# A 65-column first transform, a rearranged loading tail and filter checks moved into the mixers, in an attention and convolution network on one core

## The chip, the core and the metric

The kernel runs on one core of a Trainium2 chip. Five engines with queues of their own work side by side: PE (TensorE, matrix products), DVE (VectorE), ACT (ScalarE), POOL (GpSimd) and SP (SyncE, which here issues DMAs). An engine takes up its own instructions in order; semaphores tie the engines together. The metric is the device time of one execution in microseconds. Every operand is fp32, and each fp32 product shows in the trace as two PE records, each with a weight load before it.

## The reference, cut to what matters

The input x has 4 batches of 32 images of 128 x 128. Two layers follow each other, and each adds to x first a mixing over the image and then a recurrent network over the rows. Layer 0's mixing is an attention whose maps are spectral convolutions; layer 1's is a filtered leaky ReLU.

```python
# layer 0
x = x + conv0(ln_c(x), ...)              # the attention below
t = to_tokens(x); t = t + ffn0(ln_t(t))  # scan of yt = sigmoid(wx_t + yt @ V.T)
# layer 1
x = x + conv1(ln_c(x), bias, up, dn)     # up-filter, leaky ReLU, down-filter
t = to_tokens(x); t = t + ffn1(ln_t(t))

def codano_forward(x, ...):
    tokens = x.reshape(b * t, 1, H, W)
    tokens_norm = instance_norm(tokens, norm1_g, norm1_b)
    k = fno_layer(tokens_norm, key_w, ..., (H // 2, W // 2))
    q = fno_layer(tokens_norm, query_w, ..., (H // 2, W // 2))
    v = fno_layer(tokens_norm, value_w, ..., (H, W))
    dprod = softmax(einsum('bhtd,bhsd->bhts', qf, kf) / scale)
    attn = einsum('bhts,bhsd->bhtd', dprod, vf)
    attn = instance_norm(fno_layer(attn, proj_w, ...) + tokens, ...)
    m = fno_layer(instance_norm(attn, ...), mixer_w1, ..., norm=..., act=gelu)
    m = fno_layer(m, mixer_w2, ..., norm=...)
    return instance_norm(m, ...) + attn
```

An `fno_layer` is a 1x1 convolution, resampled to the output's shape, plus a product with weights on a few low frequencies between two Fourier transforms. Only 32 by 17 frequencies are ever used, so the transforms are products with small tables.

## The kernel before

All 128 images lie in SBUF as `XA` (partition: image row). The stages follow each other: loading and first transform with the attention scores (to about 137 us), attention applied (`mix`, `SUMS`, `NORMS`), the two mixers (`MIXERS`, an order written out by hand, run for eight chunks of four tokens), the first scan, the convolutions of layer 1 with their features, and the second scan.

**Loading.** Image loads go out on SP in pieces of eight images (512 KB, `load`). For each half batch k (16 images, eight in all) `stats(k, n)` takes row statistics on DVE (L823) and turns them into factors `r` and `nmr` (L385 to L390, L375 to L380, with one square root on ACT, L376). `transform(k)` normalises the images in place, ACT or DVE by the image's number (`normalise`, L845 and L847), multiplies each by a table of 130 columns in `cst` (L862), copies three images' results at a time from PSUM to `A1` (L863), multiplies `A1` by further tables into `pfs`, the low frequencies (L870), and into `ps_pr`, a half-size image in a rotated basis (L874, L876), which ACT copies to `Rn` (L879), and sends the normalised images to the DRAM tensor `normed` (L881).

**Scores.** `scores(b)` copies `pfs` to `FF` (L888), turns it on DVE (L889), replicates it through PE (L895, L896), multiplies it with the weights on DVE (L902 to L924), transposes on PE (L931, L932) and forms the scores `psc` (L936). `gram(b)` forms the products of `Rn` (L947, L952). `scales` prepares factors (L962 to L988), and `attend(b)` is the softmax (L1001 to L1020), which ends with one block of `CTbd`. `weights` prepares the weights (L621 to L736). Each is a generator; the loops over k step them between pieces of `transform`.

**Order.** In a `with in_order()` block every instruction of PE, DVE, ACT and POOL is tied to the one traced before it on its engine. Outside such blocks a scheduler places the instructions by a cost model, so one traced late can land early in a queue if its inputs seem to be there; `ndcm` (L717), which needs only the constants, is one. Transforms 0 and 1 and the tail are in order; transforms 2 to 7 are not. After transform 7 SP issues eight loads that bring `normed` back into `XA`, now with rows on another axis (L1071), and then runs this order:

```python
with in_order():
    for work in (scoring, extra, extra, extra, scoring, scoring, scoring, products, products, scoring, scoring,
                 scoring, scoring, scoring, extra, extra, scoring):
        step(work)
    through(scoring, extra, attend(NB - 1))
```

`extra` is `filters()`: for both of layer 1's filters it checks that the two-dimensional filter is an outer product (L759 to L785, counts in `ok`) and lays out its taps (L789 to L805). The taps go to a DRAM tensor `hankel` (L807), cleared before (L748); both are read only in layer 1. The first `mix` product (L1092) needs all of `CTbd` and the first reloaded rows.

**Mixers.** Each piece of `MIXERS` is a function with a chunk's number. M4c ends a chunk's weights on DVE (L1565, L1566), FHG transforms them back on PE (L491), Z forms the next images on DVE (L1418), g is a GELU on ACT (L1423), R adds up the result on DVE (L1586, L1587), and FS and BN take statistics (L1597, L459). The PSUM tile with the tag "t" in the pool `psf` has one buffer.

Of the kernel before, what the change touches and what calls it, by code (L numbers as in the profile page):

```python
# [26 lines left out]
F32 = mybir.dt.float32  # L27
AF = mybir.ActivationFunctionType
ALU = mybir.AluOpType
# [125 lines left out]
    IRI0.2 M4b.1 de.1 M4c.1 FHG.1 gBc.1 g3.2 Z0.2 FS2.0 Z1.2 g2.2 QG0.1 FS1.0 FS0.0 g1.2 g0.2 ST2.2 A2.2 sq2.2 FS3.0  # L155
    IRS0.1 TA1.1 ZS2.2 AF.0 sq3.2 ST0.2 QG1.1 PW.0 ZS3.2 ZD.2 A0.2 TA0.1 PF.2 sq0.2 R1a.1 sq1.2 LD2.1 FZ.2 SQ.2
    R0b.1 R0a.1 FHIa.3 R1b.1 AO.0 IRS2.1 M1.2 TA2.1 LD0.2 FHIb.3 R2b.1 XN1a.0 XN0b.0 PS.2 M2.2 TA3.1 QI0.3 XN0a.0
    PG1.2 XN1b.0 QI1.3 R2a.1 PG2.2 XT0.0 M2b.2 IRI2.3 R3a.1 R3b.1 XC0.0 XT1.0 P2.2 IRI0.3 Z2.3 M3.2 Z3.3 WX0.0 XC1.0
    P3.2 XN2a.0 al.2 Z0.3 M4a.2 g2.3 M4b.2 g3.3 Z1.3 g0.3 de.2 GB.2 M4c.2 BN0.0 g1.3 FS2.1 FS1.1 ZS2.3 ST2.3 sq1.3
    sq2.3 FHG.2 ST0.3 QG0.2 XN3b.0 IRS0.2 A2.3 A0.3 TA1.2 gBc.2 TA0.2 XN2b.0 FS3.1 PF.3 sq0.3 FS0.1 WC0.0 XT2.0  # L160
    ZS3.3 QG1.2 sq3.3 WX1.0 FZ.3 ZD.3 R1b.2 AF.1 R0b.2 IRS2.2 SQ.3 TA3.2 XC2.0 PW.1 R0a.2 PG1.3 R1a.2 M1.3 BN1.0
    LD2.2 PS.3 TA2.2 R3a.2 XN3a.0 WC1.0 M2.3 AO.1 WX2.0 R2a.2 FHIa.4 BN2.0 R3b.2 PG2.3 XN0b.1 FHIb.4 M2b.3 XT3.0
    P2.3 XN0a.1 M3.3 WC2.0 al.3 QI0.4 R2b.2 QI1.4 P3.3 XC3.0 IRI0.4 XN1a.1 XT0.1 Z1.4 M4a.3 IRI2.4 WX3.0 XN1b.1 Z0.4
    XC0.1 g1.4 M4b.3 de.3 g0.4 M4c.3 Z3.4 Z2.4 GB.3 FHG.3 BN3.0 FS3.2 g3.4 FS1.2 FS2.2 LD0.3 QG0.3 ST0.4 g2.4 FS0.2
    gBc.3 A0.4 QG1.3 ZS3.4 ZS2.4 IRS0.3 sq1.4 TA1.3 sq2.4 ST2.4 LD2.3 R1a.3 TA0.3 A2.4 WC3.0 PF.4 R1b.3 XN2b.1 FZ.4
    AF.2 ZD.4 XT1.1 sq3.4 R0b.3 WX0.1 IRS2.3 PW.2 R0a.3 SQ.4 sq0.4 PG1.4 TA2.3 XC1.1 M1.4 PS.4 BN0.1 TA3.3 AO.2 M2.4
    M2b.4 R2b.3 XN3a.1 XN2a.1 WC0.1 XT2.1 FHIa.5 R3b.3 LD0.4 R3a.3 XC2.1 P2.4 XN3b.1 XN0b.2 M3.4 PG2.4 XN0a.2 P3.4
    FHIb.5 QI0.5 QI1.5 XT3.1 WX1.1 IRI0.5 al.4 R2a.3 XN1a.2 XC3.1 BN1.1 M4a.4 Z1.5 IRI2.5 de.4 WC1.1 M4b.4 M4c.4
    XN1b.2 FS0.3 GB.4 gBc.4 WX2.1 XT0.2 BN2.1 g1.5 XN2b.2 Z3.5 WC2.1 FHG.4 FS3.3 XC0.2 QG0.4 WX3.1 FS1.3 FS2.3 QG1.4
    LD2.4 XT1.2 XN2a.2 XN3a.2 IRS0.4 XC1.2 TA1.4 BN3.1 Z2.5 TA0.4 AF.3 g2.5 Z0.5 R1b.4 XT2.2 IRS2.4 g0.5 WC3.1  # L170
    FHIa.6 sq0.5 R1a.4 R0a.4 R0b.4 WX0.2 ZS2.5 PW.3 g3.5 ZS3.5 BN0.2 TA2.4 AO.3 FHIb.6 ZD.5 ST2.5 sq2.5 FS0.4 R2b.4
    XN3b.2 ST0.5 XC2.2 sq1.5 R2a.4 sq3.5 WC0.2 A0.5 TA3.4 WX1.2 R3b.4 BN1.2 A2.5 PF.5 QI0.6 IRI0.6 XN0a.3 R3a.4
    XN0b.3 XT3.2 Z0.6 WC1.2 FZ.5 SQ.5 M1.5 QI1.6 PG1.5 XC3.2 g0.6 Z1.6 IRI2.6 PS.5 Z2.6 M2.5 g1.6 WX2.2 Z3.6 g2.6
    g3.6 P2.5 BN2.2 M2b.5 M3.5 XN1a.3 XT0.3 FS2.4 PG2.5 P3.5 FS3.4 XC0.3 ST0.6 al.5 M4a.5 WC2.2 A0.6 ST2.6 de.5
    M4b.5 M4c.5 WX0.3 A2.6 BN0.3 XN1b.3 PF.6 ZS2.6 sq0.6 ZS3.6 sq3.6 FS1.4 GB.5 FZ.6 FHG.5 WC0.3 SQ.6 QG0.5 WX3.2
    sq2.6 AF.4 IRS0.5 TA0.5 PW.4 PG1.6 sq1.6 gBc.5 XT1.3 QG1.5 M1.6 XC1.3 LD0.5 ZD.6 BN3.2 TA1.5 R0a.5 XN2a.3 R0b.5
    PS.6 LD2.5 AO.4 IRS2.5 M2.6 XN3b.3 XN2b.3 TA3.5 WC3.2 XT2.3 P2.6 M2b.6 XN3a.3 WX1.3 XC2.3 R1a.5 PG2.6 XT3.3
    TA2.5 R1b.5 FHIa.7 FHIb.7 XN0a.4 R3a.5 BN1.3 M3.6 R2a.5 XN0b.4 XC3.3 WC1.3 WX2.3 XN1b.4 QI0.7 R2b.5 XT0.4 P3.6
    QI1.7 R3b.5 al.6 BN2.3 M4a.6 de.6 XN1a.4 IRI0.7 IRI2.7 XN2b.4 XC0.4 WC2.3 Z1.7 LD0.6 M4b.6 WX3.3 g1.7 XT1.4
    M4c.6 BN3.3 FHG.6 XC1.4 WC3.3 WX0.4 Z0.7 Z2.7 FS2.5 g0.7 FS0.5 g2.7 GB.6 Z3.7 FS1.5 QG0.6 ST0.7 g3.7 BN0.4  # L180
    IRS0.6 FS3.5 A0.7 sq0.7 ZS2.7 TA1.6 ST2.7 gBc.6 ZS3.7 XN2a.4 ZD.7 WC0.4 QG1.6 A2.7 TA0.6 XT2.4 PF.7 R1b.6 sq1.7
    R1a.6 sq3.7 LD2.6 WX1.4 AF.5 FZ.7 R0a.6 SQ.7 XN3b.4 IRS2.6 PW.5 R0b.6 PG1.7 sq2.7 TA2.6 M1.7 LD0.7 XC2.4 PS.7
    AO.5 XN0a.5 XN3a.4 BN1.4 WC1.4 XN0b.5 R2a.6 M2.7 R2b.6 TA3.6 XT3.4 XN1a.5 XC3.4 WX2.4 R3b.6 M2b.7 P2.7 PG2.7
    XN1b.5 BN2.4 WC2.4 XT0.5 M3.7 WX3.4 R3a.6 al.7 P3.7 BN3.4 M4a.7 de.7 XC0.5 LD2.7 FS2.6 M4b.7 XT1.5 XN2b.5 XC1.5
    GB.7 WC3.4 M4c.7 FS3.6 XN2a.5 gBc.7 WX1.5 BN1.5 WC1.5 FS0.6 XT2.5 FHG.7 WX0.5 QG0.7 FS1.6 XN3b.5 AF.6 BN0.5
    IRS0.7 WC0.5 TA0.7 R0a.7 QG1.7 XC2.5 TA1.7 PW.6 XN3a.5 TBL.7 WX2.5 XT3.5 IRS2.7 R1a.7 AO.6 BN2.5 XN0b.6 TA2.7
    XC3.5 XN0a.6 R0b.7 WC2.5 R1b.7 XN1b.6 XT0.6 XN1a.6 XC0.6 FS1.7 FS0.7 WX3.5 AF0.7 XT1.6 BN3.5 TA3.7 XN2b.6 R2a.7
    R2b.7 XN3b.6 WC3.5 WX0.6 XN2a.6 XC1.6 XN3a.6 XT2.6 WX1.6 XC2.6 BN0.6 PW0.7 XT3.6 FS2.7 AO0.7 WC0.6 R3b.7 R3a.7
    WX2.6 BN1.6 XN02a.7 XN00a.7 FS3.7 XN00b.7 XC3.6 XN02b.7 WC1.6 WX3.6 XT02.7 XT00.7 XC02.7 XC00.7 AF2.7 WX02.7
    BN2.6 BN3.6 WC2.6 WC3.6 PW2.7 AO2.7 XN20b.7 WX00.7 XN22b.7 XN20a.7 XN22a.7 XT20.7 BN02.7 BN00.7 XC20.7 XT22.7  # L190
    XC22.7 WX20.7 BN20.7 WC00.7 WC02.7 WX22.7 BN22.7 WC20.7 WC22.7
# [15 lines left out]
C_E = 0  # L207

C_DW = C_E + 130
C_CR = C_DW + 96  # L210
C_SW = C_CR + 128
C_EH2 = C_SW + 256
# [19 lines left out]
def _constants():  # L232
    c = np.zeros((P, C_N), np.float64)
# [14 lines left out]
    basis = np.concatenate([(h2[:, None] % 2 == np.arange(2)) / np.sqrt(32), np.cos(turn) / np.sqrt(32),  # L248
                            np.sin(turn) / np.sqrt(32)], 1)
    c[:, C_E + 64 : C_E + 128] = rows.real.T @ basis  # L250
    c[:, C_E + 128 : C_E + 130] = (rows.imag.T @ basis)[:, :2]
# [3 lines left out]
    c[:, C_CR : C_CR + 64] = cols.real  # L255
    c[:, C_CR + 64 : C_CR + 128] = -cols.imag
# [30 lines left out]
def _network(  # L287
# [94 lines left out]
    def row_stats(st, n, mean, var):  # L382

        d = sm([P, NG], "rw_d")[:, :n]
        tt(mean, st[:, :, 1], st[:, :, 4], ALU.add)  # L385
        ts(mean, mean, 0.5, None, ALU.mult)
        tt(d, st[:, :, 1], st[:, :, 4], ALU.subtract)
        stt(d, d, 0.25, d, ALU.mult, ALU.mult)
        tt(var, st[:, :, 2], st[:, :, 5], ALU.add)
        stt(var, var, 1.0 / P, d, ALU.mult, ALU.add)  # L390
# [169 lines left out]
    s4 = aw.tile([P, NB], F32, name="s4")  # L560
    ndcm = aw.tile([P, 1], F32, name="ndcm")
# [28 lines left out]
    nc.sync.dma_start(cst[:, :C_SW], consts[:, :C_SW])  # L590
# [6 lines left out]
    if redo is not None:  # L597
        for k in range(2):
            F = wp.tile([2 * PAD + 1, 2, 12], F32, name=f"F{k}")
            taps_in.append(F)  # L600
            for j in range(2):
                f = up[j, 0] if k == 0 else dn[j]
                nc.gpsimd.dma_start(F[:, j, :], f[P // 2 - PAD : P // 2 + PAD + 1, :, P // 2])
    nc.sync.dma_start(cst[:, C_SW:], consts[:, C_SW:])
# [10 lines left out]
    def weights():  # L615
# [101 lines left out]
        ts(ndcm, dcm, -1.0, 1.0, ALU.mult, ALU.add)  # L717
# [21 lines left out]
    def filters():  # L739

        n = 2 * PAD + 1
# [4 lines left out]
        taps = wp.tile([1, 8, n], F32, name="taps")  # L750
        for k in range(2):
            F = taps_in[k]

            def small_(shape, name):
                return wp.tile(shape, F32, tag=name, name=name)


            fsq = small_([n, 3, 12], "fsq")
            tt(fsq[:, 0, :], F[:, 0, :], F[:, 1, :], ALU.add)  # L759
            tt(fsq[:, 1:3, :], F, F, ALU.mult)  # L760
            tt(fsq[:, 1, :], fsq[:, 1, :], fsq[:, 2, :], ALU.add)
            rsum = small_([n, 2], "rsum")
            nc.vector.tensor_reduce(rsum, F, AX.X, ALU.add)
            rows = small_([n, n, 2], "frows")
            tt(rows, ident[0:n, 0:n].unsqueeze(2).broadcast_to([n, n, 2]),
               rsum.unsqueeze(1).broadcast_to([n, n, 2]), ALU.mult)
            yield True
            p = big("ps_f")
            mm(p[:n, 0:24], ones_sq[0:n, 0:n], fsq[:, 0:2, :].rearrange("p a b -> p (a b)"), start=True, stop=True)
            mm(p[:n, 24 : 24 + 2 * n], ones_sq[0:n, 0:n], rows.rearrange("p a b -> p (a b)"), start=True, stop=True)  # L770
            sums = small_([n, 24 + 2 * n], "sums")
            nc.vector.tensor_copy(sums, p[:n, : 24 + 2 * n])
            yield True
            total = small_([n, 2], "total")
            nc.vector.tensor_reduce(total, sums[:, :24].rearrange("p (a b) -> p a b", a=2), AX.X, ALU.add)
# [1641 lines left out]
```

## Time and profile before

| what | us |
|---|---|
| three runs, median (lowest to highest) | 870.35 (870.03 to 872.82) |
| the profiled execution, its own time | 870.38 |
| its span, first to last instruction | 868.6 |
| PE, DVE, ACT, POOL busy | 750.8, 710.9, 649.4, 361.2 |
| PE's first product of transform 0 | 18.22 |
| first product of transform 1, 2 | 35.37, 47.91 |
| image reload issued, first `mix` product | 111.64, 136.83 |

PE's share of busy time is 86%, DVE's 82%, ACT's 75%: no engine alone sets the end, so gains have to be looked for in the stretches where a chain of single steps or one engine does. Matmuls are pipelined and a record of one contains its latency, so PE's real occupancy is read from runs of equal products (the length of a run of 16 against a run of 2), not from the mean duration. The page's slices of the span show PE, DVE and ACT near nine tenths in most of loading and the mixers. The time of a DMA issue and that of its landing are different records; a wait for several semaphores is put down to the one that came last.

### The profile page before, as it was taken

The page shows a single profiled execution, that of the slowest core. Times are in us where ns is not written, and L with a number is a line of the kernel's source. Part 1 is how long each engine was busy: PE and PEld are TensorE (multiplying, and loading weights), DVE is VectorE, ACT ScalarE, POOL GpSimd, SP SyncE. Part 2 cuts the span into 40 slices and gives each one's busy share as a digit, 9 for nine tenths or more (in the row PEclk, how much of TensorE's full clock was granted, in tenths as well). Part 3 has the DMA queues.
Part 4 walks back from the last instruction along what each step waited for, and adds up shares of the span by engine and source line. Part 5 has one row for each costly group of instructions (what it writes and reads, how often), then busy time and mean ns, then how long its engine had stood idle before and what let it go on. Part 6 is the DMA issues. An engine that isn't in the chain of part 4 may idle for free.

```text
span 868.6 us, 31057 instructions
## 1 busy us (share of the span) xinstructions
PE 750.8 (86%) x12550; PEld 560.5 (65%) x12550; DVE 710.9 (82%) x2330; ACT 649.4 (75%) x1669; POOL 361.2 (42%) x604
## 2 busy tenths in 40 slices
PE   1799967977878999899779979999999999998994
PEld 1566633336645555645349968888788877875994
DVE  3789668976598899899889978977878877677996
ACT  2588934585738689989779977887777887776994
POOL 2000000011435444365310016788788786961263
PEclk9799967996789899999999969999999999999998
DMA  9954992349611011120000000111111111118454
GB/s 224 260 153 94 250 366 103 137 204 276 162 51 49 26 49 35 42 73 25 25 1 1 1 3 17 40 41 40 28 41 28 41 28 40 40 40 291 172 186 148
DMA packets 105130, 83.22 MB, mean 96 GB/s; under 512 B 5457, under 2 KB 98129, under 8 KB 102865
## 3 DMA queue, kind: packets, MB, share of 16 engines
q1 hardware_dynamic: 104641, 80.86, 31.2%
q8 instruction: 101, 1.65, 0.8%
q0 software_dynamic: 288, 0.01, 0.2%
q14 instruction: 52, 0.43, 0.2%
q10 hardware_dynamic: 48, 0.26, 0.1%
HBM read 47.46 MB, written 33.66 MB: 93 GB/s over the span
## 4 chain that ended last, share of the span: by engine, by line
PE 44%; DVE 25%; ACT 14%; POOL 9%; issue 5%; DMA 1%; SPq 1%; DVEq 0%; ACTq 0%; POOLq 0%
PE ps_k L2068 5%; PE ps_scan L1915 4%; DVE XA L1587 4%; PE ps_d L2198 4%; ACT WXY L1917 4%; DVE XA L1586 4%; PE ps_st L862 3%; ACT yw L1917 3%; POOL XN L2047 3%; PE pm L1092 3%; PE ps_st L1429 3%; PE ps_r L2068 2%; PE ps_e L2205 2%; PE ps_y L1299 2%; POOL xn L2047 2%
## 5 line engine op out<-in xcount | busy, mean ns | idle before, releaser
L2188 DVE SCALAR_TENSOR_TENSOR U<-raw 128x512 f32<-128x512 f32 x128 | 89.8, 731 | 27.8 <-ACT raw L2180 27.6
L1916 DVE SCALAR_TENSOR_TENSOR ps_scan<-WXY,bs,ps_scan 128x128 f32<-128x128 f32 x376 | 105.5, 352 | 1.8 <-PE ps_scan L1915 0.8
L2068 PE MATMUL ps_k<-WXY,q 64*64 64x134 f32 x2048 | 86.0, 282 | 0.9 <-ACT WXY L2152 0.3
L2180 ACT COPY raw<-ps_k 128x512 f32<-128x512 f32 x128 | 71.0, 597 | 17.0 <-PE ps_k L2068 14.6
L2198 PEld LDWEIGHTS ps_d<-WXY,U 128*64 128x64 f32 x2048 | 66.7, 137 | 19.5 <-issue 12.1
L2047 POOL TENSOR_SCALAR XN<-XA,c_r,c_o 128x128 f32<-128x128 f32 x120 | 74.7, 631 | 5.0 <-issue 2.2
L2047 POOL TENSOR_SCALAR xn<-XA,f_r,f_o 128x128 f32<-128x128 f32 x120 | 67.2, 569 | 18.1 <-PE ps_x L2068 12.1
L2198 PE MATMUL ps_d<-WXY,U 128*64 128x67 f32 x2048 | 73.4, 224 | 1.2 <-ACT q L2211 0.9
L2068 PEld LDWEIGHTS ps_k<-WXY,q 64*64 64x64 f32 x2048 | 60.7, 135 | 6.4 <-DVE U L2188 0.8
L862 PE MATMUL ps_st<-cst,XA 128*128 128x130 f32 x256 | 42.8, 313 | 24.9 <-ACT XA L845 22.1
L2068 PE MATMUL ps_r<-WXY,XN 64*64 64x134 f32 x1024 | 59.0, 290 | 2.8 <-DVE XN L2047 1.3
L862 PEld LDWEIGHTS ps_st<-cst,XA 128*128 128x128 f32 x256 | 35.9, 212 | 29.1 <-ACT XA L845 23.1
L1644 ACT ACTIVATE xn<-XA,f_o,f_r 128x128 f32<-128x128 f32 x120 | 51.0, 489 | 4.6 <-DVE f_o L1626 3.4
L1423 ACT ACTIVATE Z<-Z,k,aB 128x128 f32<-128x128 f32 x128 | 51.0, 480 | 4.2 <-DVE Z L1418 4.0
L1586 DVE SCALAR_TENSOR_TENSOR XA<-ps_inv,r1B,xin 128x128 f32<-128x128 f32 x128 | 44.1, 345 | 8.1 <-PE ps_inv L1579 8.1
L1587 DVE SCALAR_TENSOR_TENSOR XA<-Z,gB,XA 128x128 f32<-128x128 f32 x128 | 46.3, 362 | 5.0
L2166 ACT COPY q<-ps_r 128x512 f32<-128x512 f32 x64 | 38.2, 597 | 13.2 <-PE ps_r L2068 12.8
L2027 POOL TENSOR_TENSOR c_r<-c_e,neg_half 128x16 f32<-128x16 f32 (+2 forms) x10 | 25.6, 2563 | 53.3 <-DVE c_e L2020 53.1
L506 PE MATMUL ps_inv<-invq,cst 64*128 64x512 f32 x128 | 41.4, 674 | 3.9 <-ACT invq L497 3.2
L456 PE MATMUL ps_wx<-xt,wvt 128*128 128x512 f32 x64 | 35.9, 643 | 6.7 <-ACT WXY L463 5.5
L845 ACT ACTIVATE XA<-XA,p_n,p_r 128x128 f32<-128x128 f32 x80 | 35.4, 491 | 7.6 <-DVE p_n L829 7.6
L2205 PE MATMUL ps_e<-WXY,q 128*64 128x67 f32 x1024 | 40.8, 222 | 0.0
(441 smaller groups left out, 2100.8 us busy)
## 6 DMA issues: line engine op xcount, KB each, us to landing
XA<-in_x_dram SPq DMA_DIRECT2D x16, 512.0 KB, 7.2
normed<-XA SPq DMA_DIRECT2D x8, 1024.0 KB, 6.1
XA<-normed SPq DMA_DIRECT2D x8, 1024.0 KB, 10.4
mixed<-XA SPq DMA_DIRECT2D x8, 1024.0 KB, 3.8
XA<-mixed SPq DMA_DIRECT2D x32, 256.0 KB, 5.3
xin<-in_x_dram SPq DMA_DIRECT2D x32, 256.0 KB, 3.3
turned<-XA SPq DMA_DIRECT2D x32, 256.0 KB, 2.5
out_dram<-res SPq DMA_DIRECT2D x52, 128.0 KB, 2.1
```

Source lines behind the costliest of these rows:

```text
L862: mm(p[:, i, :], XA[:, b, t0 + j + i, :], cst[:, C_E : C_E + 130], start=True, stop=True)
L1423: nc.scalar.activation(z, z, AF.Gelu, bias=k1, scale=aB[:, j : j + 1])
L1586: stt(a, p2[c, b][:, i], r1B[:, j : j + 1], xin[c, b - b % 2][:, b % 2, i], ALU.mult, ALU.add)
L1587: stt(a, Z[c][:, b, i], gB[c][:, n : n + 1], a, ALU.mult, ALU.add)
L1916: stt(p4, WX[:, :, h, :], s[:, 0:1], p4, ALU.mult, ALU.add)
L1917: nc.scalar.activation(dst, p4, AF.Sigmoid, bias=s[:, 1:2])
L2047: e.tensor_scalar(dst, src_, r, o, ALU.mult, ALU.add)
L2068: m = mm(dst, data, taps, start=(n == 0 and (i, j) not in last), stop=(n == 1), skip_group_check=True)
L2180: nc.scalar.copy(raw[u, k], banks["k", u][:, k])
L2188: stt(U[u][:, k].rearrange("p k s m -> p (k s m)"), v, SLOPE, v, ALU.mult, ALU.max)
L2198: mm(p[HALVES[s], m, b, REACH[k]], U[v][:, b, k, s, HALVES[m]], DR[:, k, REACH[k]], start=(m == 0 and b == 0 and k == 0), stop=(k == 1), s ...
L2205: mm(p[HALVES[j], b * P : b * P + P][:, REACH[m]], q3[v - 1][:, m, b, HALVES[j]], DC[:, m, REACH[m]], start=(b == 0 and m == 0), stop=(m = ...
```

## The change

The first product of a transform has 65 columns instead of 130: the table (`C_F`) holds the cosine and sine parts in a real basis, from which the low frequencies and the half-size image are both formed. Three banks of 7, 6 and 3 images replace six of up to three, and six images are normalised ahead instead of three. The products into `pfs` and `ps_pr` read `A1` as `p k j`, with the images innermost, so that their results stand in the order in which `FF` and `Rn` keep them; four products form `ps_pr` instead of three. The tables of this stage are a tile of their own (`tables`, loaded first), and `cst` keeps the rest. From the third half batch on ACT normalises 12 of 16 images, in the last one 8.

`ndcm` is computed in order behind transform 0. `FF` has a buffer of its own. `scales` runs beside transform 6 and the softmaxes of batches 0 and 1 beside transform 7, which is now in order, with the `FF` copy before its last products. The tail is rearranged. `filters` moves, as nine pieces FL, into `MIXERS`; clearing of `hankel` is traced ahead of the loops.

```diff
-    nc.sync.dma_start(cst[:, :C_SW], consts[:, :C_SW])
+    nc.sync.dma_start(tables, consts[:, C_N:])
...
-        def normalise(k, images):
+        def normalise(k, i):
...
+            if i % 8 not in ((1, 4, 6) if k < 2 else (1, 3, 5, 6) if k == 2 * NB - 1 else (2, 6)):
...
-            A1 = a1p.tile([P, HB, 130], F32, name="A1")
-            normalise(k, range(0, 3))
-            for n, j in enumerate(range(0, HB, 3)):
-                m = min(3, HB - j)
-                normalise(k, range(j + 3, min(j + 6, HB)))
-                p = psa.tile([P, 3, 130], F32, tag="st1", name="ps_st1")
-                for i in range(m):
-                    mm(p[:, i, :], XA[:, b, t0 + j + i, :], cst[:, C_E : C_E + 130], start=True, stop=True)
-                nc.scalar.copy(A1[:, j : j + m, :], p[:, :m])
-                yield True
+            A1 = a1p.tile([P, HB, 65], F32, name="A1")
+            for i in range(AHEAD):
+                normalise(k, i)
+            for i in range(HB):
+                if i in (0, 7, 13):
+                    p = psa.tile([P, 7, 65], F32, tag="st1", name="ps_st1")
+                    j = i
+                if i + AHEAD < HB:
+                    normalise(k, i + AHEAD)
+                mm(p[:, i - j, :], XA[:, b, t0 + i, :], tables[:, C_F : C_F + 65], start=True, stop=True)
+                if i in (6, 12, 15):
+                    nc.scalar.copy(A1[:, j : i + 1, :], p[:, : i + 1 - j])
+                if i in (2, 4, 6, 9, 12, 15):
+                    yield True
...
+                    a = A1[:, :, (slice(33, 48) if part else slice(1, 17)) if half else
+                           (slice(48, 32, -1) if part else slice(17, 1, -1))].rearrange("p j k -> p k j")
+                    mm(pfs[b][32 * g : 32 * g + 32, HB - a.shape[1] :, t0 : t0 + HB], tables[:, w : w + 32], a,
+                       start=(part == 0), stop=True, skip_group_check=(part == 1))
+            yield True
+            p = big("ps_pr").rearrange("p (k j) -> p k j", j=HB)
+            for q, k0, k1, w, c in ((0, 2, 32, 0, 2), (64, 0, 32, 0, 32), (0, 0, 2, 64, 0), (0, 0, 1, 128, 64)):
+                mm(p[q : q + 64, k0:k1], tables[:, C_CR + w : C_CR + w + 64],
+                   A1[:, :, c : c + k1 - k0].rearrange("p j k -> p k j"), start=(w < 128), stop=True,
+                   skip_group_check=(w == 128))
...
-            dst = Rn[:, :, b * NT + t0 : b * NT + t0 + HB].rearrange("p h j -> p j h")
-            nc.scalar.copy(dst, p)
+            nc.scalar.copy(Rn[:, :, n0 : n0 + HB], p)
...
-            FF = sp.tile([P, 2, 16, NT], F32, tag="KM", name="FF")
+            FF = sp.tile([P, 2, 16, NT], F32, tag="FF", name="FF")
-            nc.scalar.copy(Fe.rearrange("p k t -> p t k"), pfs.pop(b))
+            nc.scalar.copy(Fe, pfs.pop(b))
...
+            ts(ndcm, dcm, -1.0, 1.0, ALU.mult, ALU.add)
             ahead = stats(2, 2)
...
-        for k in range(2, 2 * NB):
+        for k in range(2, 2 * NB - 1):
...
-                step(ahead, prepare if k > 2 else None, scoring, softmax if k > 5 else None)
+                step(ahead, prepare if k > 2 else None, scoring, scaling if k > 5 else None)
...
+        through(scaling)
         with in_order():
-            for work in (scoring, extra, extra, extra, scoring, scoring, scoring, products, products, scoring, scoring,
-                         scoring, scoring, scoring, extra, extra, scoring):
+            last, features = transform(2 * NB - 1), scores(NB - 1)
+            for n, _ in enumerate(last):
+                step(scoring, softmax)
+                if n == 6:
+                    next(features)
+            for h in range(0, P, ROWS):
+                nc.sync.dma_start(XR[:, h : h + ROWS, :], normed[:, h : h + ROWS, :])
+            through(scoring)
+            products = gram(NB - 1)
+            for work in (features, softmax, features, features, products, softmax, products, features, softmax, features,
+                         softmax, features, features, features, softmax, features, softmax):
                 step(work)
-            through(scoring, extra, attend(NB - 1))
+            through(features, softmax, attend(NB - 1))
...
-    IRI0.2 M4b.1 de.1 M4c.1 FHG.1 gBc.1 g3.2 Z0.2 FS2.0 Z1.2 g2.2 QG0.1 FS1.0 FS0.0 g1.2 g0.2 ST2.2 A2.2 sq2.2 FS3.0
+    IRI0.2 M4b.1 de.1 M4c.1 FL.0 FHG.1 gBc.1 FL.0 g3.2 Z0.2 FS2.0 Z1.2 g2.2 QG0.1 FS1.0 FS0.0 g1.2 g0.2 ST2.2 A2.2
...
```

The other seven FL stand after PF.2, R3a.1, M4c.2, PF.3, R2a.2, M4c.3 and PF.4; the first, fifth start a filter's four steps (preparation on DVE; two products on PE and the copy `sums` on DVE; the check; the taps), and the ninth is the DMA of the taps. `row_stats` (L385 to L390) computes the same in another order.

## The prediction

> **What bounds the kernel now.** I read the waits first, then busy time by stretch, then the timeline at the ends of loading. Columns of the table: length, then busy time (instructions) of PE, its weight loads, DVE, ACT and POOL, granted clock, DMA.
>
> ```profile
> 13.00:18.20 5.20, 0.00 (x0) 0.00 (x0) 1.06 (x7) 0.53 (x2) 0.38 (x3) 1.00 1.16 304
> 18.20:35.40 17.20, 11.68 (x71) 8.93 (x71) 9.71 (x57) 8.19 (x22) 0.00 (x0) 0.79 1.15 279
> 47.90:102.30 54.40, 49.63 (x485) 35.60 (x486) 49.28 (x204) 48.09 (x121) 0.00 (x0) 1.00 0.63 157
> 111.64:136.80 25.16, 13.29 (x153) 8.12 (x152) 16.05 (x70) 6.94 (x16) 1.46 (x2) 0.61 0.82 334
> ```
>
> Loading ends when L1092 starts, at 136.8 us. Four regimes: nothing to multiply until 18.2; the first transform; transforms 2 to 6, 10.9 us each, with three engines at 88 to 91% and none alone the bound; and a tail of 25 us that is one chain of short steps. The head, in the timeline (start, length):
>
> ```profile
> 12.07 0.17 DVE L379 TENSOR_TENSOR rq_d<-rq_d,rq_e 128x16 f32<-128x16 f32 x1
> 17.07 0.15 DVE L717 TENSOR_SCALAR ndcm<-cst 128x1 f32<-128x1 f32 x1 [4.82 <-DMA cst<-in_consts_dram]
> 17.14 0.28 DVE L380 SCALAR_TENSOR_TENSOR p_r<-rq_d,p_r 128x16 f32<-128x16 f32 x1
> ...
> 17.67 1.65 ACT L845 ACTIVATE XA<-XA,p_n,p_r 128x128 f32<-128x128 f32 x4 [6.12 <-DVE p_n L829]
> ...
> 18.22 2.97 PE L862 MATMUL ps_st<-cst,XA 128*128 128x130 f32 x12 [18.22 <-ACT XA L845]
> ```
>
> `ndcm`, which transform 0 doesn't use, sits in DVE's queue in front of the factors that all wait for. The tail:
>
> ```profile
> 112.72 0.71 DVE L889 STREAM_TRANSPOSE FF<-FF 128x512 f32<-128x512 f32 x1 [1.36 <-ACT FF L888]
> ...
> 117.03 1.27 PE L895 MATMUL ps_fr<-FF,WXY 32*128 32x272 f32 x2
> ...
> 129.57 0.18 DVE L772 COPY sums<-ps_f 7x38 f32<-7x38 f32 x1 [2.26 <-PE ps_f L770]
> ...
> 132.10 0.27 DVE L1001 TENSOR_TENSOR Pm<-wqk,pg 128x128 f32<-128x128 f32 x1
> ```
>
> PE could take L895 at 113.4 but stands behind a transpose that waits for a softmax until 116.6; the filter work holds the last softmax from 129.6 to 132.1.
>
> [...] L862 and L1429 both load 128 columns and move 130 and 64: runs of 16 take 2.39 and 2.00 us, so half the columns don't halve it. [...] (columns: total, mean ns):
>
> ```profile
> L1560 DVE TENSOR_TENSOR G<-G,al 128x256 f32<-128x256 f32 x8 | 3.3, 416 | 0.1
> L1561 DVE SCALAR_TENSOR_TENSOR G<-WXY,sc,G 128x256 f32<-128x256 f32 x8 | 5.3, 662 | 0.3
> L463 ACT COPY WXY<-ps_wx 128x512 f32<-128x512 f32 x28 | 16.3, 581 | 15.5 <-DVE bn L459 15.4
> L879 ACT COPY WXY<-ps_pr 128x512 f32<-128x512 f32 x8 | 8.3, 1041 | 5.7 <-PE ps_pr L876 5.6
> L874 PE MATMUL ps_pr<-A,cst 128*64 128x512 f32 x32 | 9.9, 629 | 0.0
> ```
>
> L1561 reads elements 128 bytes apart, L879 writes them 512 apart; L463 writes runs of four. On PE no row before has such a read.
>
> **The change, part by part.** The sum is made against the profiled execution, 870.38 us (span 868.6; median of three 870.35, so the same).
>
> *Head.* `ndcm` goes behind transform 0's statistics, where `cst` has long landed. DVE's 4.82 us stall goes. Next late are the tables of the transform: they are issued at 1.84, behind 1 MB of images that had landed by 8.4, so about 9.5; the factors are ready near 12.6. **-4.9.** Images of the second half were issued before `cst`, landed at 17.05, so they don't stop it.
>
> *Transform 0.* Six images are normalised ahead instead of three, so the 13 DVE steps of `weights` (22.6 to 25.2) no longer keep PE, idle for 2.4 us. ACT's square root now comes before the Rn copy (DVE waited 3.1 us for it; ACT's next normalise gains 34.82-33.64 = 1.2). The Rn copy falls from 1.04 to 0.58 us (L463's time). Sum 4.0; clock at 0.79 and extra queueing, I take **-3.5**, and for transform 1 **-0.5**.
>
> *PE per transform.* Each image's two passes: 0.136 us a pass by runs of L862 ((2.39-0.49)/14), 0.107 by L1429; 32 passes, -0.9. Two small matmuls of ps_pr more, +0.2. Then the unknown: the moving operand of ps_pf and ps_pr is read k-major out of A1, elements 260 bytes apart. Per transform 4 rounds of 256 columns and 2 of 512 (column groups run side by side), 2048 columns at some 0.83 ns (L874: four in 1.08 us, two by two, is 1.05 ns with its ends). From below: nothing, since a column per 0.83 ns might still be fed. From above: the trace's 1.7 ns an element: L1561 less some 225 fixed over 256; L879 less L463 adds 0.9 to ACT's 0.83. I take 1.7, since both engines with strides land there and PE reads the same memory: +1.75 us. So PE +1.05.
>
> *ACT per transform.* A1 copies: five of 483 and one of 266 become about 537, 483 and 320 (the slope between these rows): -1.3; Rn -0.46; the FF copy, every second, -0.45; two more normalises, +0.8. Net -1.2. DVE -0.6. FF has a buffer of its own, a wait less.
>
> *Transforms 2 to 6.* PE rises from some 9.1 to 10.1 of 10.9 us, while ACT and DVE fall and six images ahead loosen their coupling: I take +0.2 each, **+1.0**. If PE isn't fed, +1 each.
>
> *Transform 7 and tail.* It carries two softmaxes now, **+0.5**. The tail along its new order from the FF copy: copy 0.6, transpose 0.7, ps_fr with copies 2.3, FK 0.3, products 1.4, second softmax step 0.8, products 1.4, scaling 0.4, differences 1.4, transposes with copies 3.4, scores 1.5, and the last softmax 4.7 (132.1 to 136.8): 18.9 against 25.2. In-order queues won't give it all: **-5.0**. The image reload needs some 19 us plus 4.7 for the last write, and moves with transform 7; it ends about when mixing begins, which eats it in pieces, so it stays hidden.
>
> *Filters into the mixers.* DVE's some 40 small steps: 3.4 us a filter by the timeline (0.75+0.2+1.6+0.9), 6.9. Cover there is thin: DVE 61.3 and PE 61.6 busy of 70 between 250 and 320 us. Worse is the wait at `sums`: the second FL stands behind FHG.1's 64 matmuls on PE, and DVE's L1418 stands behind it.
>
> ```profile
> 253.75 0.22 DVE L1566 TENSOR_SCALAR G<-G 128x128 f32<-128x128 f32 x1
> 254.47 2.91 PEld L491 LDWEIGHTS ps_inv<-cst,G 32*64 32x64 f32 x64 [1.50 <-issue]
> 254.48 3.15 PE L491 MATMUL ps_inv<-cst,G 32*64 32x128 f32 x64
> 254.58 0.75 DVE L1418 SCALAR_TENSOR_TENSOR Z<-XA,sc,ps_inv 128x512 f32<-128x512 f32 x1 [0.60 <-PE ps_inv L506]
> ```
>
> DVE would go on at some 258 instead of 254.6; Z and then GELU wait for it. Holes follow (1.3 us at 264.4, 3.4 at 287.7). Bounds: 0 if all falls into holes, 11 (6.9, 3.5 and a second wait of 1) if nothing does. I take **+5.0**.
>
> Their last step is a DMA of the taps on POOL's queue, 0.56 us of issue; POOL is busy 33 of 70 us there, and `YT`'s clearing no longer stands behind it (1.9 us of POOL, on no chain): nothing.
>
> *The rest.* Order inside `row_stats`, the constants' layout: nothing. Hankel's zeros move on SP from 69.86, where SP spent 11.8 us on them behind a store of single elements, to behind the 8 image loads that keep SP until 25.6. They pass `md`'s store there; if they hold SP, `md`, landing near 38.6, would be late by 1 or 2 us for products that I expect from 40.7. I take nothing.
>
> Sum: -4.9-3.5-0.5+1.0+0.5-5.0+5.0 = -7.4, so **863.0 us**.
>
> **Rivals.**
> (a) PE isn't slowed by strides. Transforms 2 to 6 then gain 0.7 each instead of losing 0.2 (4.5), transform 1 another 0.5, transform 7 gains 0.5 instead of losing it (1.0), the tail another 0.5: 863.0 - 6.5 = 856.5. For: an fp32 column takes PE 0.83 ns[...]. Against: the two strided rows.
> (b) The filters eat the gain: DVE is the mixers' chain, all 11 us land, and 1 us of the tail's gain fails: 870. For: DVE idle only 1.3 us in 300 to 325. Against: the holes named.
> (c) Slower: PE pays 2.5 ns a column[...]. That is +3.4 us a transform, PE 11.8 us of work in 10.9, so about 13 at today's share; transforms 2 to 6 cost +10.5, transforms 1 and 7 +1.7 each, the first gains 2.5, the tail 4.2: -4.9-2.5+1.7+10.5+1.7-4.2+5.0 = +7.3, 877.7. It decides from about 2.1 ns a column. For: no row shows strides with several groups. Against: nothing costs over 1.75 here.
>
> **How the numbers follow.** Forecast 0.42, (a) 0.27, (b) 0.17, (c) 0.14. The forecast's own range is 858 to 869 (the filters 0 to 11). The range, 854 to 874, takes in all but most of (c) and the far side of (a). This kernel's runs tell 0.3%, 2.6 us, from no change. Faster: 0.8 of the forecast, all of (a), a quarter of (b): 0.65. Same: 0.17 of the forecast, half of (b), a little of (c): 0.18. Slower: 0.17.
>
> **What would show it.** PE's first matmul near 13.3 us; L862's successor with 65 columns at 0.107 us a pass; ps_pf's 16 passes in about 1.9 us instead of 1.07 (1.1 means (a), 2.8 means (c)); copies of Rn and FF at 0.58; mixing started near 124.5; the stretch from there to the scan longer by 5. It is wrong if DVE finds another early wait, or if the tail stays at 25 us.

## The result and the profile after

The changed kernel takes 898.12 us (median of four runs, 894.66 to 901.32) where the kernel before takes 870.19 beside it: 1.0314 times as long, 95% interval 1.0268 to 1.0361. Forecast was 863.0, with a range of 854 to 874. The profiled execution took 899.38 us, its span is 897.6 against 868.6. Seven stations, read from both traces, split these 29.0 us:

| stretch | before | after | difference |
|---|---|---|---|
| start to PE's first product | 18.22 | 12.86 | -5.4 |
| transform 0 | 17.15 | 15.38 | -1.8 |
| transform 1 (to the first product of transform 2) | 12.54 | 15.43 | +2.9 |
| transforms 2 to 6 | 54.4 | 71.8 | +17.4 |
| transform 7, to the FF copy of the last image | 9.3 | 18.0 | +8.7 |
| tail, FF copy to the first `mix` product | 25.2 | 17.3 | -7.9 |
| first `mix` product to the first scan product on WXY | 330.6 | 345.7 | +15.1 |
| from there to the end | 401.2 | 401.1 | 0 |

The transforms from the second on lose, and so does something between mixing and scan. The tail's gain has to be read together with transform 7's loss, since work moved from the one to the other: 34.5 us before, 35.3 after. Busy time by stretch of the changed kernel, columns as in the prediction (length; PE, weight loads, DVE, ACT, POOL; granted clock; DMA):

```profile
12.90:28.20 15.30, 13.86 (x72) 10.23 (x72) 10.78 (x60) 6.48 (x19) 0.38 (x3) 1.00 1.09 291
43.70:115.50 71.80, 69.91 (x470) 45.85 (x470) 45.11 (x185) 45.08 (x113) 1.79 (x3) 0.77 0.58 148
134.90:150.80 15.90, 9.44 (x140) 6.59 (x139) 9.94 (x29) 5.26 (x14) 0.90 (x1) 0.73 1.01 424
```

In the second line PE is busy all but 1.9 us, and DVE and ACT, which were at 90% before, at 63%. PE has become the bound of transforms 2 to 6, although the columns of its passes were halved. The third figure from the end tells why to look further: the granted clock is 0.77, where the same stretch had 1.00 before. Cut into steps of 4 us, the clock is not 0.77 anywhere for long: it stands at 1.00 from 56 to 72 us and from 88 to 104, and at 0.50 from 44 to 52, 76 to 84 and 108 to 112. The 1.00 of the first line is not borne out by the work in it: the weight loads of `ps_st` from 12 to 23 us took 333 ns in the median, as they did at 0.50 (333 from 76 to 84 us), and 192 at 1.00 (56 to 72 us).

The head does what was forecast. Timeline of the head:

```profile
11.89 0.18 DVE L386 SCALAR_TENSOR_TENSOR p_r<-rq_d,p_r 128x16 f32<-128x16 f32 x1
12.31 0.88 ACT L785 ACTIVATE XA<-XA,p_n,p_r 128x128 f32<-128x128 f32 x2 [1.16 <-DVE p_n L770]
12.86 0.48 PE L804 MATMUL ps_st<-tables,XA 128*128 128x65 f32 x1 [12.86 <-ACT XA L785]
```

The 4.82 us behind `ndcm` are gone. The loss of the mixers stands in DVE's waits from 205 to 330 us (waiting line, releaser; us in total, times, longest):

```profile
DVE sums L1299 <- PE ps_f L1297: 14.1, 2, 10.3
DVE XA L1593 <- PE ps_inv L1586: 3.6, 2, 2.9
```

At two copies of 7 x 38 elements DVE stood idle for 14.1 us, where the stage lost 15.1. PE's timeline at the second one shows what it stood behind:

```profile
304.43 3.68 PE L1436 MATMUL ps_st<-cst,Z 128*128 128x64 f32 x16
308.03 2.08 PE L512 MATMUL ps_inv<-invq,cst 64*128 64x512 f32 x4
310.04 3.39 PE L1586 MATMUL ps_inv<-XA,gI 128*128 128x512 f32 x4
313.36 1.08 PE L484 MATMUL ps_pf<-A,cst 128*32 128x128 f32 x32
314.37 0.21 PE L1296 MATMUL ps_f<-fsq,ones_sq 7*7 7x24 f32 x2
```

DVE had been idle since 304.3. The two tiny products it waited for are queued behind 10 us of PE's other work. Part of that length is the clock, which was 0.50 from 300 to 312 us: in e9 below, at 1.00 from 294 us on, the same stretch of queue took 6 us, the first of these lines 2.00 instead of 3.68, and the wait was 5.5 (9.3 for the two).

### The profile page after: what moved, and what is told of

It is laid out like the page before. It is cut to its first block, busy times and chain, and to the rows that moved or that the text cites. A ratio compares the mean times of both kernels' runs of the same rounds, so it can differ in the third digit from the quotient of the medians.

```text
span 897.6 us, 31052 instructions
## 1 busy us (share of the span) xinstructions
PE 788.0 (88%) x12566; PEld 576.3 (64%) x12566; DVE 710.0 (79%) x2322; ACT 642.4 (72%) x1655; POOL 363.4 (40%) x604
## 4 chain that ended last, share of the span: by engine, by line
PE 47%; DVE 27%; ACT 12%; POOL 7%; issue 4%; DMA 1%; another core or an unknown queue 0%; SPq 0%; DVEq 0%; ACTq 0%; POOLq 0%
PE ps_scan L1927 5%; PE ps_st L804 5%; DVE XA L1594 5%; PE ps_k L2080 4%; DVE XA L1593 4%; PE ps_d L2210 4%; ACT WXY L1929 4%; PE pm L1038 3%; POOL XN L2059 3%; DVE f_st L1604 2%; PE ps_r L2080 2%; PE ps_pf L815 2%; PE ps_pr L820 2%; PE ps_inv L497 2%; POOL xn L2059 2%
## 5 line engine op out<-in xcount | busy, mean ns | idle before, releaser
L2192 ACT COPY raw<-ps_k 128x512 f32<-128x512 f32 x128 | 71.2, 599 | 17.4 <-PE ps_k L2080 14.8
L804 PE MATMUL ps_st<-tables,XA 128*128 128x65 f32 x256 | 52.4, 370 | 15.2 <-ACT XA L785 15.2
L804 PEld LDWEIGHTS ps_st<-tables,XA 128*128 128x128 f32 x256 | 47.2, 275 | 24.1 <-ACT XA L785 17.4
L1927 PE MATMUL ps_scan<-y,wvt 128*128 128x128 f32 x246 | 40.5, 281 | 0.0
## 6 DMA issues: line engine op xcount, KB each, us to landing
XA<-normed SPq DMA_DIRECT2D x8, 1024.0 KB, 10.6
```

The source lines that it names most:

```text
L804: mm(p[:, i - j, :], XA[:, b, t0 + i, :], tables[:, C_F : C_F + 65], start=True, stop=True)
L1927: mm(p4, self.t[:, 1, :], prev, start=True, stop=True)
L2192: nc.scalar.copy(raw[u, k], banks["k", u][:, k])
```

## The experiments

Medians of all; the ratio is to the kernel before, run beside each. The other columns are from the one profiled execution of each, in us: the first `mix` product, the length of transforms 2 to 6, the stretch from the first `mix` product to the first scan product, and the mean granted clock from 52 to 100 us. In e3 (886.90) and e8 (868.91) that execution was slower than the median, in e10 (870.45) the quickest of nine.

| run | us | ratio (95%) | mix | transforms 2 to 6 | mix to scan | clock |
|---|---|---|---|---|---|---|
| before | 870.19 | | 136.8 | 54.4 | 330.6 | 1.00 |
| changed | 898.12 | 1.0314 (1.0268 to 1.0361) | 150.8 | 71.8 | 345.7 | 0.84 |
| e1_rows | 892.93 | 1.0275 (1.0186 to 1.0365) | 145.0 | 64.9 | 344.5 | 0.85 |
| e2_sums_late | 889.07 | 1.0180 (1.0120 to 1.0239) | 152.1 | 73.6 | 334.9 | 0.76 |
| e3_both | 882.35 | 1.0140 (1.0085 to 1.0195) | 142.9 | 64.3 | 341.2 | 0.86 |
| e4_head | 865.61 | 0.9930 (0.9903 to 0.9958) | 133.2 | 58.0 | 331.1 | 1.00 |
| e5_pad130 | 864.21 | 0.9917 (0.9896 to 0.9938) | 127.1 | 54.3 | 333.4 | 1.00 |
| e6_six_copies | 898.96 | 1.0294 (1.0226 to 1.0362) | 159.9 | 76.9 | 337.5 | 0.61 |
| e7_before_65 | 888.90 | 1.0204 (1.0140 to 1.0267) | 157.8 | 72.5 | 329.3 | 0.65 |
| e8_filters_early | 861.60 | 0.9876 (0.9811 to 0.9941) | 132.6 | 57.8 | 333.7 | 0.93 |
| e9_pad_only | 885.86 | 1.0170 (1.0139 to 1.0202) | 140.2 | 61.2 | 342.2 | 1.00 |
| e10_cols98 | 877.37 | 1.0068 (1.0048 to 1.0089) | 133.5 | 59.6 | 334.1 | 0.93 |
| e11_filters_earlier | 862.56 | 0.9885 (0.9854 to 0.9916) | 130.2 | 55.9 | 330.1 | 0.93 |

### Strides or clock: e1, and the two losses together: e2, e3

e1 gives A1 the order in which PE reads it, and leaves the striding to ACT:

```diff
-A1 = a1p.tile([P, HB, 65], F32, name="A1")
+A1 = a1p.tile([P, 65, HB], F32, name="A1")
-nc.scalar.copy(A1[:, j : i + 1, :], p[:, : i + 1 - j])
+nc.scalar.copy(A1[:, :, j : i + 1].rearrange("p k j -> p j k"), p[:, : i + 1 - j])
```

The products then read `A1[:, 1:17]` and the like, without a rearrangement.

> The changed kernel with A1 laid out column by column (65 x 16 instead of 16 x 65): the three copies out of PSUM write it strided, and PE reads it in order. Theory 'stride': the moving reads of A1 at a distance of 65 elements cost transforms 2 to 7 their time. The 16 passes of ps_pf fall from 2.2 to about 1.1 us and the ps_pr passes from 2.1 to about 1.3 us, 1.9 us a transform over eight transforms, most of it on the chain: mixing starts near 138 instead of 150.8, total 884 to 887 (12 to 14 us less). Rival 'clock': what costs the time is the granted TensorE clock (0.77 against 1.00 over transforms 2 to 6), whatever the layout; the clock stays near 0.77 and the total falls by under 6 us, to 892 or more. Rival 'copies': ACT's strided copies take twice their time (0.5 to 1.0 us for 455 elements) and become the bound: total within 3 us of the changed kernel.

5.2 us came back by the medians (the intervals overlap), the size the clock rival gave, and the clock stayed where it was. In the trace transforms 2 to 6 are 6.9 us shorter, of the 17.4 lost. ACT's copies did double (455 elements 528 to 927 ns, 195 elements 322 to 490), without becoming the bound. ps_pf's passes gained less than was expected of them: their median went from 689 to 634 ns only, while the shortest fell from 639 to 366. Passes read in order took this long at half clock: sixteen of them 1.92 us from 79.99 us, at 0.50, and 1.06 from 65.32, at 1.00.

e2 puts a step between the products and the copy of `sums`, and moves the copies on in the mixers' order:

```diff
+            yield True
             sums = small_([n, 24 + 2 * n], "sums")
-...R2b.1 XN1a.0...   PF.3 FL.0 sq0.3...   TA3.2 XC2.0 PW.1...        LD2.2 PS.3
+...R2b.1 FL.0 XN1a.0...   PF.3 sq0.3...   TA3.2 XC2.0 FL.0 PW.1...   LD2.2 FL.0 PS.3
```

> The changed kernel with the copy of sums split from the matmuls of ps_f in the mixers' order: DVE comes to it some 20 to 40 instructions later, when PE has done them. Theory 'in-order wait': the two copies of sums, at which DVE stood idle 3.81 and 10.33 us (14.1 together), are the whole loss of the mixers; from the first mixing matmul to the first scan matmul the time falls from 345.7 to about 331, total about 884. Rival 'more work': the filters' 48 small DVE instructions themselves (about 8 us) or a lower clock in the mixers cost it; the idle time goes and the stage falls by under 6 us, total 892 or more.

9.05 us came back by the medians; 889.07 lies between the 884 of the theory and the 892 of its rival. DVE's timeline passes the copy without a stop:

```profile
314.64 0.69 DVE L465 BATCH_NORM_STATS2 bn<-ps_wx 128x6 f32<-128x512 f32 x1
315.25 0.17 DVE L1300 COPY sums<-ps_f 7x38 f32<-7x38 f32 x1
315.35 0.33 DVE L1594 SCALAR_TENSOR_TENSOR XA<-ps_inv,r1B,xin 128x128 f32<-128x128 f32 x1
```

From mixing to scan it is 334.9 us instead of 345.7 (331 expected; 330.6 before). So the waits were 10.8 of the 15.1 by this pair of traces. DVE was busy 290.2 us in the stage against 285.0 before, so the checks' own work is the likely rest. The stage is not the same to a us in every trace: with this edit it is 341.2 in e3, at a mean clock of 0.89, and 333.4 in e5, at 0.93; here it was 0.92.

> Both edits of the two kernels before it in one. If the losses are two and independent, the gains add: total about 870 (869 to 874), mixing from near 138, first scan matmul near 469. If they overlap or the clock is the cause of the loading's loss, 878 or more.

882.35 lies 15.8 below the changed kernel, near the 14.2 of the two alone, and in the branch "overlap or the clock"; the first alone was small. Some 12 us were missing. In the profiled execution, whose span was 16.5 us above that of the kernel before, 6.1 of them are lost up to mixing and 10.6 from there to the scan.

### The head alone: e4

The kernel before with its `ndcm` line moved behind transform 0's statistics.

> The kernel before with one line moved: ndcm is computed on DVE behind transform 0 instead of ahead of the key's factors. Theory: PE's first matmul comes at about 13 us instead of 18.2, and transform 2 starts 4 to 5 us sooner; most of it reaches the end, total 865 to 867. Rival: the inputs' arrival or DVE's statistics set transform 1 or 2, and under 1.5 us is left at the end, total 869 to 871.

First product at 13.2, 865.61 us, 0.70% faster, in the range given. By the interval that is 3.7 to 8.5 us, where the head gained 5.0; in the trace 3.6 of these are left at mixing. It shows also that the clock of transforms 2 to 6, 1.00 in its trace, doesn't fall because the loading begins earlier.

### What lowers the clock: e5, e6, e7

e5 is e3 with passes of 130 columns, of which 65 are used:

```diff
-if i in (0, 7, 13):
-    p = psa.tile([P, 7, 65], F32, tag="st1", name="ps_st1")
+if i % 3 == 0:
+    p = psa.tile([P, 3, 130], F32, tag="st1", name="ps_st1")
-mm(..., tables[:, C_F : C_F + 65], ...)
+mm(..., tables[:, C_F : C_F + 130], ...)
-if i in (6, 12, 15):
-    nc.scalar.copy(..., p[:, : i + 1 - j])
+if i % 3 == 2 or i == HB - 1:
+    nc.scalar.copy(..., p[:, : i + 1 - j, :65])
```

> e3_both with every pass of the first transform streaming 130 columns again (65 of its table and the 65 that lie behind them, which nobody reads), copied out of PSUM in groups of three images, 65 columns of each. PE gets more work, nothing else. [...] with 130 the clock of transforms 2 to 6 goes back to 0.95 or more (0.77 in the changed kernel), mixing starts near 135 instead of 142.9, total 874 to 877. Rival 'work': the clock dips have another cause (DMA, the copies, the run) and stay; PE streams twice the columns, total 884 or more.

e6 is the same with 65 columns streamed: this number alone differs between the two.

> The kernel e5_pad130 with its passes back at 65 columns, six copies of three images as there: what the six copies alone do. [...] the clock stays near 0.77 in transforms 2 to 6 and the total near e3_both's 882 (879 to 886). Rival: the copies' rhythm is what matters, and the total is within 2 us of e5_pad130.

e7 is the kernel before, streaming 65 columns and copying them twice:

```diff
-mm(p[:, i, :], ..., cst[:, C_E : C_E + 130], ...)
+mm(p[:, i, :65], ..., cst[:, C_E : C_E + 65], ...)
-nc.scalar.copy(A1[:, j : j + m, :], p[:, :m])
+nc.scalar.copy(A1[:, j : j + m, :].rearrange("p m (r c) -> p m r c", r=2),
+               p[:, :m, :65].unsqueeze(2).broadcast_to([P, m, 2, 65]))
```

> The kernel before with each pass of its first transform cut to 65 of its 130 columns and nothing else: ACT copies the 65 columns twice, so that all other instructions keep their sizes. Left out: the second half of the transform's columns, so the attention's inputs are other numbers. [...] the granted clock of transforms 2 to 6 falls from 1.00 to 0.8 or less, and the kernel is slower with less work, 874 to 885. Rival 'work': less streaming, the same or up to 4 us faster, 866 to 871.

e7 decides it: half the streaming taken out of a kernel, with its copies as long as before (484 ns against 483), costs 18 us, as much as transforms 2 to 6 lose in its trace (72.5 us against 54.4). Busy time from 52 to 100 us, first of the kernel before, then of e7:

```profile
52.00:100.00 48.00, 43.24 (x433) 30.93 (x436) 43.87 (x185) 41.90 (x106) 0.00 (x0) 1.00 0.57 138
```

```profile
52.00:100.00 48.00, 45.33 (x362) 33.15 (x362) 34.65 (x149) 31.99 (x78) 0.00 (x0) 0.65 0.36 81
```

PE is busy longer, gets through 362 instead of 433 instructions, and its clock is 0.65. e6 and e5 in the same stretch:

```profile
52.00:100.00 48.00, 46.43 (x329) 30.94 (x329) 26.09 (x123) 26.88 (x70) 0.00 (x0) 0.61 0.36 82
```

```profile
52.00:100.00 48.00, 44.46 (x456) 31.51 (x453) 32.50 (x138) 40.80 (x107) 0.00 (x0) 1.00 0.64 156
```

With one number doubled, PE does 456 instructions instead of 329 and the kernel takes 34.8 us less. The passes themselves, e7 first, then e5 (shortest, median, longest ns):

```profile
L862 PE MATMUL ps_st<-cst,XA x256: 222/417/477, 18.0 to 130.6; 128*128 128x65 f32 x128
```

```profile
L804 PE MATMUL ps_st<-tables,XA x256: 274/276/588, 12.8 to 107.1; 128*128 128x130 f32 x128
```

The median pass of 65 columns is longer than that of 130. e7 went beyond the 885 it was given, e5 below its 874: both ways the effect was larger than I thought. e6 missed its expectation by more: 899, not 882. So the six short copies in place of three cost 16.6 us at 65 columns, with the clock at 0.61 instead of e3's 0.86. The columns streamed are the same in both, so they are not all that sets the clock; how the copies lower it further was not taken apart.

### Stride at full clock, and how many columns: e9, e10

e9 is the changed kernel with e5's 130 columns only.

> The changed kernel with one thing altered, its first transform's passes at 130 columns as in e5_pad130; A1 stays image by image, so PE's reads of it stay strided, and sums stays where it was. [...] the clock of transforms 2 to 6 is back at 0.95 or more and the stage 6 us or more shorter than the changed kernel's; with the mixers' loss of 9 and the strided reads still there, total 876 to 884. And at full clock the strided reads must show their own price: the passes of ps_pf at about 640 ns as against e5_pad130's 379, some 1.1 us a transform. Rival: the strided reads alone hold PE back[...], total 890 or more.

One edit takes 12.3 us off the changed kernel: clock 1.00, mixing 10.6 us sooner. The total, 885.86, lies 1.9 us above the range given. ps_pf's passes now show the stride alone, e9 first, then e5:

```profile
L815 PE MATMUL ps_pf<-A,tables x128: 595/671/754, 23.2 to 121.3; 128*32 128x256 f32 x96, 128*32 128x240 f32 x32
```

```profile
L815 PE MATMUL ps_pf<-A,tables x128: 365/379/405, 22.5 to 108.4; 128*32 128x256 f32 x96, 128*32 128x240 f32 x32
```

671 against 379 ns. Four runs now make a square of the two faults, transforms 2 to 6 in us:

| | 65 columns | 130 columns |
|---|---|---|
| strided reads | 71.8 (changed) | 61.2 (e9) |
| ordered reads | 64.9 (e1) | 54.3 (e5) |

In this stage they add: 10.6 us for the columns, with either kind of reads, and 6.9 for the reads, with either number of columns. Each figure is from one trace; e2 and e3, which load as the changed kernel and e1 do, have 73.6 and 64.3, so they hold to some 2 us. The medians of whole kernels look otherwise (the 130 columns gave 12.3 with strided reads, e9, and 18.1 with ordered ones, e3 to e5), but 7.8 us of the step from e3 to e5 lie between mixing and scan in their traces, where the edit changes nothing.

> e5_pad130 with 98 columns a pass instead of 130 (65 used). Where between 65 and 130 the clock falls isn't known. If what counts is the streamed share of PE's time in proportion, 98 lies half way, and the clock of transforms 2 to 6 is 0.85 to 0.95, total 870 to 878. If it is enough that the streaming outlasts the weight load beside it, the clock stays at 0.95 or more and the total within 2 us of e5_pad130's 864. If it is not, as with 65, 882 or more.

98 columns of 130 give 877.37, in the range of "in proportion": at 98 columns the clock was 0.93, at 130 it had been 1.00. One run between the two doesn't show a proportion. The times spread more than elsewhere (870.45 to 879.80), and the profiled execution, with 0.93, was the quickest of them.

### Filters in the loading: e8, e11

Both are the changed kernel with ordered A1 and 130 columns, the checks stepped through transforms 4 to 6 (e8) or 2 to 4 (e11) of the loading. This is e11's edit; e8 has `k > 3` in the last line:

```diff
-step(ahead, prepare if k > 2 else None, scoring, scaling if k > 5 else None)
+step(ahead, prepare if k > 2 else None, scoring, scaling if k > 5 else None,
+     extra if 1 < k < 5 else None)
```

> The changed kernel with A1 column by column, 130 columns a pass as in e5_pad130, and the filters' checks stepped through transforms 4 to 6 instead of the mixers. Theory: DVE and PE have room there, so the loading is as long as e5_pad130's (mixing from 134 to 137), and the mixers return to the kernel before's 330.6 us from first mixing matmul to first scan matmul: total 866 to 871. Rival: the checks delay the statistics or the feature maps on DVE's queue in the loading, 4 us or more, total 873 or more.

> e8_filters_early with the filters' checks stepped through transforms 2 to 4 instead of 4 to 6, further from the end of the loading. If the checks hold up anything at the late transforms (its profile had the clock at 0.59 from 92 to 100 us), 858 to 861; if their place is of no account, within 2 us of 861.6; if DVE is fuller in transforms 2 and 3, where it was busy without a break from 44 to 56 us in the changed kernel, 864 or more.

Both beat the two kernels of the case and don't differ from each other by what can be told: "their place is of no account" stands. e8's median lies below the 866 to 871 I gave it. Its trace doesn't say why, being of the slowest of its four executions (859.25 to 868.91), which lies in that range. In e11 mixing to scan is 330.1 us, that of the kernel before, so the checks are out of it; but mixing starts 3.1 us later than in e5, so that the traces of the two end within 0.4 us of each other, and their intervals overlap. That the loading is a cheaper place for the checks than e5's order of the mixers isn't shown.

## Why the prediction was wrong

*Head, -4.9.* Right: -5.4 in the trace, and 0.70% at the end when made alone (e4).

*Transform 0 and 1, -3.5 and -0.5.* -1.8 and +2.9. The clock of transform 1 was 0.77, where it had been 0.88. With 130 columns and ordered reads (e5) the two are -3.4 and +0.6, so transform 0's gain is there once both faults are gone.

*Transforms 2 to 6, +1.0.* This is the step that failed: +17.4. By the square above some 10.6 of it are the columns and 6.9 the strides. The first term that was mis-sized is the pass of ps_st, "0.107 by L1429; 32 passes, -0.9". At full clock it came near, at half clock it did not (first and last line at 1.00, the two between at 0.50):

```profile
60.28 0.44 PE L804 MATMUL ps_st<-tables,XA 128*128 128x65 f32 x2
78.32 0.69 PE L804 MATMUL ps_st<-tables,XA 128*128 128x65 f32 x2
47.55 4.10 PE L804 MATMUL ps_st<-tables,XA 128*128 128x65 f32 x18
61.01 2.73 PE L804 MATMUL ps_st<-tables,XA 128*128 128x65 f32 x22
```

By the prediction's own way, a long run against a run of 2, that is 0.115 us a pass at 1.00 and 0.213 at 0.50, and the products into `ps_fr` took 736 ns in the mean at 0.50 (76 to 84 us) against 441 at 1.00 (88 to 104). The working took the clock of 1.00 in the stretch 47.90 to 102.30 for a fact of the stage. It was the doing of the 130 columns that the change took away: e7 shows it without the rest of the change (1.00 fell to 0.65 from 52 to 100 us), e9 by giving them back (0.84 rose to 1.00). The trace of the kernel before held a warning. The 2.00 us of L1429, from which 0.107 comes, is one of its runs; the next one, of the same 16 passes of 64 columns, took nearly twice as long, with PE busy throughout and at a granted clock of 0.50:

```profile
209.40 2.00 PE L1429 MATMUL ps_st<-cst,Z 128*128 128x64 f32 x16
212.58 3.67 PE L1429 MATMUL ps_st<-cst,Z 128*128 128x64 f32 x16 [1.18 <-ACT Z L1423]
```

In the changed kernel's trace the clock stands at 0.50 or at 1.00: 0.50 from 29.6 to 36.4 us, 0.99 to 43.3, 0.50 to 53.5, 1.00 to 74.0, and so on. Idle time doesn't go with the low level: PE was busy 46.43 of 48 us at 0.61 (e6) and 43.24 at 1.00 (before). By these runs a busy PE can lose its clock when less is streamed beside the same weight loads: 45.33 us busy at 0.65 in e7, with 65 columns and the same 256 loads of 128. As an estimate from the lengths of records before (378 ns for 256 columns, 592 for 512, so 0.84 ns a column), a run of 65-column passes streams for 54 of the 115 ns of each pass, and one of 130 columns for 109 of 136. What exactly the clock follows, the runs leave open. One more thing fits, as a coincidence in time only: the five stretches at 0.50 between 29 and 132 us end at 36.4, 53.5, 87.6, 114.9 and 132.0 us, 1.4 to 3.6 us after the start of a run of ps_pf's passes of 256 columns (34.7, 52.1, 84.1, 113.2, 130.3).

*Strides.* Their price for PE was sized well: "ps_pf's 16 passes in about 1.9 us" were 2.2 to 2.3, between that and rival (c)'s 2.8, against 1.06 in order at full clock (e5), and ps_pr's eight passes 2.1 against 1.21. That is some 2.0 us a transform for the forecast's 1.75. PE pays for strided reads, as DVE and ACT do in the rows that the prediction shows (L1561 662 ns where L1560 takes 416, L879 1041 where L463 takes 581); e9 shows it, with 671 ns a pass against 379. The working's 225 ns fixed are an estimate; the same operation on elements in order took 345 to 362 ns for 128 columns and 731 to 741 for 512 in that trace (L1586, L1587, L2188, L1418), which leaves 213 to 239. What failed is that slack would hide most of it, "+0.2 each": 6.9 us over five transforms, 1.4 each, arrived (e9 to e5). Rival (c) had the right side and a part of the cause: e1 took the strides away and kept 10.5 of the 17.4 us.

*ACT's copies.* Rn 586 ns and FF 570 to 590, as forecast (0.58).

*Transform 7, +0.5, and tail, -5.0.* Taken alone they are +8.7 and -7.9, but together +0.8, where -4.5 was forecast. The clock is the smaller part: at 1.00 throughout transform 7, e5 takes 15.8 + 17.4 = 33.2 us and e9 19.1 + 17.4 = 36.5, against 34.5 before. So most of the tail's gain was paid for in transform 7, which carries the softmaxes now and is in order. Its timeline in the changed kernel:

```profile
121.00 0.29 DVE L946 TENSOR_TENSOR Pm<-Pm,psc 128x128 f32<-128x128 f32 x1 [7.20 <-PE psc L880]
122.18 0.34 DVE L787 TENSOR_SCALAR XA<-XA,p_r,p_n 128x128 f32<-128x128 f32 x1
125.06 0.36 PE L957 MATMUL ps_pt<-ident,Pm 128*128 128x128 f32 x1 [2.06 <-DVE Pm L954]
125.22 1.39 PE L804 MATMUL ps_st<-tables,XA 128*128 128x65 f32 x6
```

DVE's normalising (L787) stands behind a softmax step that waits 7.20 us for the scores, and the passes of transform 7 behind a transpose that waits for the softmax. No run puts the softmaxes back, so how the loss divides between these waits stays open. The reload stays hidden.

*Filters, +5.0 with 11 as the upper end.* +15.1. The first wait was found and sized (3.5 us; 3.81 measured). The second, "a second wait of 1", was 10.33: I did not read what PE has in its queue where the second filter's products stand, and half clock lengthened it (5.5 in e9). e2 shows that the waits, and not the checks' own work, were most of it.

e5, in which the clock is restored, the reads ordered and the waits gone, takes 864.21 us. That this is near 863.0 doesn't confirm the sum: it is another kernel, in which transforms 2 to 6 and the tail with transform 7 come out otherwise than forecast, and the filters cost 2.8 us instead of 5.0.

## What to carry to other kernels

When a change takes streaming away from PE, read the granted clock of the stage as a result of the work, not as a given (65 columns less a pass took it from 1.00 to 0.65 in e7): look in the profile for runs of products as short as those left over, at what clock they ran, and try the padded form. A read of PSUM placed in an in-order queue cost what the producing engine had queued ahead of it (10.33 us here, behind some 10 us of PE's work), so look at that queue at each such place, not at the first one. Two faults in one stage are told apart by four runs and the length of that stage, not by medians of the whole kernel. Where work moves from one stretch to the next, judge the sum of both.

## What the runs showed that I had not expected

The recorded length of a pass of 65 columns with a weight load of 128 was 417 ns in the median (e7), that of one of 130 columns 276 (e5). A number of columns in between counted too: 65, 98 and 130 gave 898.96, 877.37 and 864.21 us in otherwise like kernels with six copies (e6, e10, e5); with three copies 65 columns took 882.35 (e3). At half clock weight loads lengthened as well, from 191 ns in the median before to 333 in e7. A strided pass hardly felt the clock: in the changed kernel the 16 passes of ps_pf took 674 ns in the median at 1.00 (from 64.5 us) and 684 at 0.50 (from 84.1 us), where ordered ones take 379 (e5) and 634 (e1).
